# A projection in two halves with a PSUM bank of its own, and unread matrix products at four places, in a network of attention, two Sobel layers and a recurrence

## The chip, the cores and the metric

The kernel runs on one core of one Trainium2 chip. The metric is the device time of one execution in microseconds (us). A core has five engines that run side by side and wait for each other through semaphores: TensorE (PE) multiplies matrices and writes only into PSUM, VectorE (DVE) and ScalarE (ACT) work element by element and can read PSUM, GpSimd (POOL) works element by element but only in SBUF, and SyncE (SP) issues transfers. Each engine takes its instructions in the order in which they stand in the program. TensorE's clock can be granted at full or at half speed.

## The reference, cut to what matters

The input is one image of 256 x 256 pixels with 32 channels. Four layers follow each other; each takes the group norm of the running sum and adds its result to it.

```python
x = x + attention(group_norm(x))     # layer 0
x = x + sobel(group_norm(x))         # layer 1
x = x + sobel(group_norm(x))         # layer 2
x = x + recurrence(group_norm(x))    # layer 3

# layer 0: the axis that is attended over has length 1, so the softmax is 1
mn = layer_norm(m) * ln_gamma + ln_beta       # over the 32 channels
v = mn @ Wv                                   # 32 -> 256
g = sigmoid(mn @ Wg)                          # 32 -> 256
out = (g * v) @ Wo + bo                       # 256 -> 32

# layers 1, 2: 3x3 mean, the two Sobel gradients, root of the sum of squares
out = sqrt(grad_x**2 + grad_y**2 + 1e-6)
```

Layer 3 runs a two-layer gated recurrence of 128 units over 256 columns, for 256 rows at once.

## The kernel before

**Layout.** `xa` and `xb` hold the image in SBUF as 64 blocks of 128 partitions (4 columns of pixels by 32 channels) by 256 rows of pixels. Two neighbouring blocks are a pair of 128 x 512 values, which fills one PSUM bank as fp32; there are 32 pairs (`NST`) and eight banks. An fp32 matrix product appears in the trace as two passes, each with its own weight load.

**Unread products.** At several places the kernel multiplies the identity with a constant tile and never reads the result (`junk`, `px`): `busy` (line 139) in the group norm, line 271 and line 296 in the layer norm, and `busy` (line 921) ahead of the recurrence.

**Layer norm (lines 232 to 298).** First the values are centred and their variances gathered into one bank. Then the reciprocal root `rstd` has to be spread over the channels: for each of the 32 pairs a product `pb` (line 278) takes one of four groups of 32 partitions of `rstd` and fills a bank. `pairs` goes round the four groups, so that neighbouring products lie in different row groups of TensorE. DVE multiplies (line 285), then ACT and POOL in turn apply gamma and beta (lines 287 and 291). The pool `ps_sp` has eight banks; behind the last pair stand four unread products of 256 columns.

**Attention (lines 303 to 366).** The order is written out by hand (`tc.manual_schedule`). For a pair `i` and a half `u % 2` of the 256 hidden channels, each of the four pixel columns `j` needs a value product `pv` and a gate product `pg`. Both take 32 rows of TensorE, those of column `j`. `together` issues two `pv` products and two `pg` products of a later half, then the two sigmoids on ACT (line 328) and the two multiplications `o = pv * sg` on DVE (line 331). It is called twice for each `u`, four times for each pair. The pools are rings: `ps_g` and `ps_v` have four banks each, and a product waits until the bank that it takes over has been read. After the four calls of pair `i`, `project(i - 1)` multiplies the eight `o` tiles of the pair before with `Wo`: for each half four products of 32 columns side by side, added up in one bank, which it takes from the ring of `pg`. ACT adds the bias (line 345), POOL adds the result into `xa` (line 347), and DVE later takes statistics of it (line 350).

**Sobel layers (lines 380 to 538).** Each step of a pair has a due time in a list; the list is sorted and worked off in that order. For a pair `k` the products are `centre` and `edges` (for each of the two gradients `which`), into the tiles `pg0` and `pg1` of the pool `ps_s`, three banks each. Then follow `square`, `total`, `root`, `residual` and `statistics`. Behind each layer stands a `group_norm`: DVE combines the statistics, TensorE makes two small products (`pm`, `pv`) with unread ones around them, and the result is the scale and bias of the next layer.

**Recurrence.** It too is sorted by due times: `project` for step 0 at -1e5, then `busy` with six unread products at -1e4, then step after step with a period of 8.4.

Of the kernel before, what the change touches and what calls it, by code (L numbers as in the profile page):

```python
# [10 lines left out]
F32 = mybir.dt.float32  # L11
# [3 lines left out]
PSUM = bass.MemoryType.PSUM  # L15

S = 256
T = 256
C = 32
J = 4  # L20
NB = T // J
P = 128
# [36 lines left out]
def net_kernel(  # L59
# [20 lines left out]
    nc = tc.nc  # L80
# [13 lines left out]
    ident = cp.tile([P, P], F32, name="ident")  # L94
    make_identity(nc, ident)
    kt = cp.tile([P, NK, P], F32, name="kt")
# [31 lines left out]
    wo = cp.tile([P, D // P, C], F32, name="wo")  # L128
    nc.gpsimd.dma_start(out=wo, in_=w_o.rearrange("(k p) c -> p k c", p=P))

    NST = NB // 2
# [62 lines left out]
    with tc.tile_pool(name="nat", bufs=3) as natp, tc.tile_pool(  # L194
        name="ps_in", bufs=4, space=PSUM
# [31 lines left out]
    pairs = [(g * KS + ks, g, ks) for ks in range(KS) for g in range(4)]  # L227
# [4 lines left out]
    with tc.tile_pool(name="ln", bufs=4) as lnp:  # L232
        rstd = lnp.tile([P, 2 * S], F32, name="rstd", bufs=1)
        with tc.tile_pool(name="ps_ln", bufs=6, space=PSUM) as ps_ln, tc.tile_pool(
            name="ps_var", bufs=1, space=PSUM
        ) as ps_var:
            cen = lnp.tile([P, P], F32, name="cen", bufs=1)
            nc.vector.tensor_scalar(cen, kt[:, K_CEN, :], gn[0], None, ALU.mult)
            pcb = ps_var.tile([P, 1], F32, name="pcb")
            nc.tensor.matmul(pcb, lhsT=kt[:, K_CEN, :], rhs=gn[1], start=True, stop=True)  # L240
            cb = lnp.tile([P, 1], F32, name="cb", bufs=1)
            nc.vector.tensor_copy(cb, pcb)
            pvar = ps_var.tile([P, 2 * S], F32, name="pvar")
            sqs = {}

            def variance(k, g, ks):
                nc.tensor.matmul(
                    pvar[g * C : (g + 1) * C, :],
                    lhsT=avg[:, ks].rearrange("p k j -> p (k j)"),
                    rhs=sqs.pop(k),  # L250
                    start=ks == 0,
                    stop=ks == KS - 1,
                )

            for i, (k, g, ks) in enumerate(pairs):
                pc = ps_ln.tile([P, 2 * S], F32, name="pc")
                nc.tensor.matmul(pc, lhsT=cen, rhs=pair(xa, k), start=True, stop=True)
                sqs[k] = lnp.tile([P, 2 * S], F32, name="sq", bufs=10)
                nc.scalar.activation(sqs[k], pc, AF.Square, bias=cb)
                nc.vector.tensor_scalar(pair(xb, k), pc, cb, None, ALU.add)  # L260
                if g == 3 and ks:
                    for q in pairs[i - 7 : i - 3]:
                        variance(*q)
            for q in pairs[-4:]:
                variance(*q)
            std = lnp.tile([P, 2 * S], F32, name="std", bufs=1)
            nc.scalar.activation(std, pvar, AF.Sqrt, bias=ln_eps)
            table(AF.Sigmoid, std[:, 0:1])
            nc.vector.reciprocal(rstd, std)
            for _ in range(9):  # L270
                nc.tensor.matmul(
                    pvar[:, 0:S], lhsT=ident, rhs=kt[:, 0:2, :], start=True, stop=True
                )
        with tc.tile_pool(name="ps_sp", bufs=8, space=PSUM) as ps_sp:
            for i, (k, g, ks) in enumerate(pairs):
                rows = slice(g * C, (g + 1) * C)
                pb = ps_sp.tile([P, 2 * S], F32, name="pb")
                nc.tensor.matmul(
                    pb,
                    lhsT=spread[rows, ks * J : (ks + 1) * J, :].rearrange("p j c -> p (j c)"),  # L280
                    rhs=rstd[rows, :],
                    start=True,
                    stop=True,
                )
                nc.vector.tensor_mul(pair(xb, k), pair(xb, k), pb)
                if i % 2:
                    nc.scalar.activation(
                        pair(xb, k), pair(xb, k), AF.Identity, scale=gamma4, bias=beta4
                    )
                else:  # L290
                    nc.gpsimd.tensor_scalar(
                        pair(xb, k), pair(xb, k), gamma4, beta4, ALU.mult, ALU.add
                    )
            junk = ps_sp.tile([P, 2 * S], F32, name="pb")
            for _ in range(4):
                nc.tensor.matmul(
                    junk[:, 0:S], lhsT=ident, rhs=kt[:, 0:2, :], start=True, stop=True
                )

    stats = new_stats()
    with tc.tile_pool(name="at", bufs=3) as atp, tc.tile_pool(
        name="ps_g", bufs=4, space=PSUM
    ) as ps_g, tc.tile_pool(name="ps_v", bufs=4, space=PSUM) as ps_v:
        gates, gated = {}, {}

        def inner(w, u, j, ps):
            i, half = divmod(u, 2)
            k = pairs[i][0]  # L310
            rows = slice(j * C, (j + 1) * C)
            mn = xb[rows, 2 * k : 2 * k + 2, :].rearrange("p b s -> p (b s)")
            nc.tensor.matmul(  # L313
                ps, lhsT=w[rows, half * P : (half + 1) * P], rhs=mn, start=True, stop=True
            )
            return ps

        def together(values, gates_of):

            pvs = {k: inner(wv4, *k, ps_v.tile([P, 2 * S], F32, name="pv")) for k in values}  # L320
            pgs = {
                k: inner(wg4, *k, ps_g.tile([P, 2 * S], F32, name="pg"))
                for k in gates_of
                if k[0] < 2 * NST
            }
            for k, pg in pgs.items():
                gates[k] = sg = atp.tile([P, 2 * S], F32, name="sg", bufs=8)
                nc.scalar.activation(sg, pg, AF.Sigmoid)  # L328
            for k, pv in pvs.items():
                gated[k] = o = atp.tile([P, 2 * S], F32, name="o", bufs=17)  # L330
                nc.vector.tensor_mul(o, pv, gates.pop(k))  # L331

        def project(i):
            po = ps_g.tile([P, 2 * S], F32, name="pg")
            for half in range(2):
                for j in range(J):
                    nc.tensor.matmul(
                        po[j * C : (j + 1) * C, :],
                        lhsT=wo[:, half, :],
                        rhs=gated.pop((2 * i + half, j)),  # L340
                        start=half == 0,
                        stop=half == 1,
                    )
            r = atp.tile([P, 2 * S], F32, name="r", bufs=2)
            nc.scalar.activation(r, po, AF.Identity, bias=bo4)
            dst = pair(xa, pairs[i][0])
            nc.gpsimd.tensor_add(dst, dst, r)

        def statistics(i):
            nc.vector.bn_stats(stats[:, i, :], pair(xa, pairs[i][0]))  # L350

        with tc.manual_schedule():
            together((), [(0, j) for j in range(J)])
            together((), [(1, j) for j in range(2)])
            for i in range(NST):
                for u in (2 * i, 2 * i + 1):
                    if i >= 3 and u % 2:
                        statistics(i - 3)
                    together([(u, 0), (u, 1)], [(u + 1, 2), (u + 1, 3)])
                    together([(u, 2), (u, 3)], [(u + 2, 0), (u + 2, 1)])  # L360
                if i >= 1:
                    project(i - 1)
            table(AF.Sqrt, one)
            for i in range(NST - 1, NST):
                project(i)
            for i in range(NST - 3, NST):
                statistics(i)
    lw = ctx.enter_context(tc.tile_pool(name="lw", bufs=1))
# [11 lines left out]
    def sobel_layer(src, dst, scale, bias, between):  # L380
# [152 lines left out]
        with tc.manual_schedule():  # L533
            for _, k, part, args in todo:
                part(k, *args)
                if part is statistics and between:
                    between.pop(0)(lambda: flat(ps_s.tile([P, 2, S], F32, name="pg1")))
        stack.close()
# [239 lines left out]
def recurrence(tc, out, ident, weights, inputs, general):  # L778
# [39 lines left out]
    def at(when, what, *args):  # L818
        todo.append((when, len(todo), what, args))

    def project(l, h, t):

        if t >= T:
            return
        zz = v["zz", l, h] = ps_zz.tile([P, 4 * H], F32, name=f"zz{l}{h}")
        rows = slice(l * X1, l * X1 + KX)
        x = inputs.of(t, rows, slice(h * P, (h + 1) * P))
        nc.tensor.matmul(zz, lhsT=x, rhs=fx[rows, l, :], start=True, stop=l == 0 and t == 0)  # L828
# [125 lines left out]
        at(((k - inputs.NX + 1) * inputs.XT * J + 2.0) * PERIOD, inputs.load, k)  # L954
    for h in range(2):
        at(-1e5, project, 0, h, 0)
    at(-1e4, busy, 6)
    at(PLAN[1, 1]["x"] - PERIOD, project, 0, 0, 1)
    at(PLAN[1, 1]["x"] - PERIOD, busy, 2)
    for t in range(T):  # L960
# [52 lines left out]
```

## Time and profile before

| What | us |
| --- | --- |
| Median of three runs (2828.97 to 2829.38) | 2829.04 |
| The profiled execution | 2832.39 |
| its span, first to last instruction | 2830.50 |
| load and transposition, first group norm (0 to 38) | 38.0 |
| layer norm up to the spreading (38 to 82) | 44.0 |
| layer norm, spreading (82 to 103.5) | 21.5 |
| attention, up to the next group norm (103.5 to 323.9) | 220.4 |
| group norm and first Sobel layer (323.9 to 473) | 149.1 |
| group norm and second Sobel layer (473 to 619.9) | 146.9 |
| group norm and weights of the recurrence (619.9 to 629.6) | 9.7 |
| recurrence (629.6 to 2830.5) | 2200.9 |

The profile is that of one execution, so its own time is shown beside its span; the difference is what lies before the first and behind the last instruction. An engine is busy while one of its instructions runs. Overlapping instructions of one engine count once, and TensorE's passes overlap, so that a PE that is busy all the time need not work at its peak. The granted clock is a share of full speed. In a timeline each line gives the start, the time that the group of equal instructions covers, engine, line, operation, the tiles written and read, the number, and in brackets the idle time of the engine before it with what ended it.

### The profile page before, as it was taken

What the parts mean: (1) busy time and instruction counts of PE and PEld (TensorE: products, weight loads), DVE (VectorE), ACT (ScalarE), POOL (GpSimd) and SP (SyncE); (2) the same over time, 40 slices, a digit from 0 to 9 for tenths busy, and PEclk for the clock granted to TensorE, in tenths of its full rate; (3) what the DMA queues carried; (4) which work ended last, traced back from release to release, by engine and by line L of the source; (5) the groups of instructions that cost most, each with busy time, mean ns of one, the idle gap of its engine ahead of it and who ended that gap; (6) DMA issues with size and microseconds to landing.
All of it is one profiled execution on the core that took longest, in us unless ns stands there. A gap on an engine that the chain in (4) does not pass through costs nothing.

```text
span 2830.5 us, 38940 instructions
## 1 busy us (share of the span) xinstructions
PE 2785.1 (98%) x9709; PEld 1051.1 (37%) x9709; DVE 2494.4 (88%) x7272; ACT 2379.3 (84%) x6980; POOL 1299.9 (46%) x1295
## 2 busy tenths in 40 slices
PE   7999999999999999999999999999999999999998
PEld 4433434343333333333333333333333333333332
DVE  6788798978999999999999999999999999999997
ACT  5677676768988888888888888888888888888887
POOL 2211375654444444444444444444444444444443
PEclk9899999999999999999999999999999999999999
DMA  3000000010000000000000000000000000000000
GB/s 136 1 1 1 16 1 1 1 23 6 16 12 12 12 12 12 12 12 12 12 14 12 12 12 12 12 12 12 12 12 12 12 12 14 16 15 12 5 5 8
DMA packets 94337, 38.41 MB, mean 14 GB/s; under 512 B 74852, under 2 KB 91269, under 8 KB 94104
## 3 DMA queue, kind: packets, MB, share of 16 engines
q1 hardware_dynamic: 92612, 34.61, 5.3%
q8 instruction: 82, 1.34, 0.2%
q14 instruction: 151, 1.24, 0.1%
q10 hardware_dynamic: 692, 0.93, 0.1%
q0 software_dynamic: 800, 0.30, 0.0%
HBM read 10.63 MB, written 8.39 MB: 7 GB/s over the span
## 4 chain that ended last, share of the span: by engine, by line
PE 76%; DVE 1%; ACT 0%; issue 0%; POOL 0%; DVEq 0%; POOLq 0%; ACTq 0%
PE zz L853 34%; PE zz L828 19%; PE zz L848 15%; PE pt L910 5%; PE px L933 1%; PE px L930 1%; DVE ve L866 0%; PE px L924 0%; POOL rs L869 0%; ACT sq L861 0%; ACT ga L842 0%; DVE c L890 0%; DVE h L905 0%; DVE fc L894 0%; DVE c L898 0%
## 5 line engine op out<-in xcount | busy, mean ns | idle before, releaser
L869 POOL TENSOR_TENSOR rs<-ve,mhalf 128x4 f32<-128x4 f32 x1024 | 1037.5, 1013 | 1153.5 <-DVE ve L866 1153.5
L853 PE MATMUL zz<-wc,hT 128*128 128x512 f32 x2040 | 1100.3, 621 | 0.5 <-DVE hT L914 0.5
L842 ACT ACTIVATE ga<-zz,rs 128x128 f32<-128x128 f32 x3072 | 927.1, 366 | 32.0 <-POOL rs L869 13.1
L866 DVE TENSOR_REDUCE ve<-sq 128x4 f32<-128x516 f32 x1024 | 707.2, 691 | 123.8 <-ACT sq L861 61.1
L861 ACT ACTIVATE sq<-zz 128x512 f32<-128x512 f32 x1024 | 609.4, 595 | 126.4 <-PE zz L853 116.1
L828 PE MATMUL zz<-fx,xt 33*128 33x512 f32 x2048 | 583.1, 642 | 0.5 <-DVE e L710 0.5
L853 PEld LDWEIGHTS zz<-wc,hT 128*128 128x128 f32 x2040 | 324.0, 188 | 554.3 <-DVE c L898 288.1
L848 PE MATMUL zz<-wc,hT 128*128 128x512 f32 x1024 | 525.0, 594 | 0.0
L902 ACT ACTIVATE th<-c 128x128 f32<-128x128 f32 x1024 | 318.1, 311 | 89.9 <-DVE c L898 80.8
L842 ACT ACTIVATE go<-zz,rs 128x128 f32<-128x128 f32 x1024 | 390.4, 381 | 0.0
L890 DVE TENSOR_TENSOR c<-ga 128x128 f32<-128x128 f32 x1024 | 295.8, 289 | 39.2 <-ACT ga L842 25.2
L910 PEld LDWEIGHTS pt<-ident,h 128*128 128x128 f32 x1024 | 142.8, 139 | 502.1 <-DVE h L905 501.5
L914 DVE COPY hT<-pt 128x128 f32<-128x128 f32 x1024 | 292.6, 286 | 26.0 <-PE pt L910 4.0
L910 PE MATMUL pt<-ident,h 128*128 128x128 f32 x1024 | 299.5, 292 | 8.1 <-DVE h L905 8.1
L905 DVE TENSOR_TENSOR h<-go,th 128x128 f32<-128x128 f32 x1024 | 291.9, 285 | 11.8 <-ACT th L902 1.5
L894 DVE TENSOR_TENSOR fc<-ga,c 128x128 f32<-128x128 f32 x1020 | 297.5, 292 | 0.6 <-ACT ga L842 0.6
L898 DVE TENSOR_TENSOR c<-c,fc 128x128 f32<-128x128 f32 x1020 | 288.1, 282 | 6.8
L828 PEld LDWEIGHTS zz<-fx,xt 33*128 33x128 f32 x2048 | 156.3, 185 | 258.9 <-ACT go L842 193.7
L331 DVE TENSOR_TENSOR o<-pv,sg 128x512 f32<-128x512 f32 x256 | 158.1, 681 | 43.6 <-PE pg L313 37.7
L848 PEld LDWEIGHTS zz<-wc,hT 128*128 128x128 f32 x1024 | 162.3, 198 | 70.8 <-issue 40.8
L328 ACT ACTIVATE sg<-pg 128x512 f32<-128x512 f32 x256 | 138.6, 599 | 31.4 <-PE pg L313 26.7
L313 PE MATMUL pv<-xb,wv 32*128 32x512 f32 x512 | 156.5, 620 | 0.0
(154 smaller groups left out, 2174.5 us busy)
## 6 DMA issues: line engine op xcount, KB each, us to landing
xt<-xa SPq DMA_DIRECT2D x256, 64.0 KB, 2.0
nat<-in_x_dram SPq DMA_DIRECT2D x16, 512.0 KB, 7.9
out_dram<-st SPq DMA_DIRECT2D x254, 32.0 KB, 1.6
wc<-in_L_conv_W_cell_dram SPq DMA_DIRECT2D x2, 512.0 KB, 4.4
kt<-in_consts_dram ACTq DMA_DIRECT2D x1, 832.0 KB, 5.8
wv<-in_L_conv_Wv_dram POOLq DMA_DIRECT2D x4, 32.0 KB, 5.1
wg<-in_L_conv_Wg_dram POOLq DMA_DIRECT2D x4, 32.0 KB, 6.7
gamma<-in_L_conv_ln_gamma_dram POOLq DMA_DIRECT2D x4, 0.1 KB, 5.9
```

Source lines behind the costliest of these rows:

```text
L828: nc.tensor.matmul(zz, lhsT=x, rhs=fx[rows, l, :], start=True, stop=l == 0 and t == 0)
L842: nc.scalar.activation(dst, gates(x, g), func, scale=scale)
L848: nc.tensor.matmul(get("zz"), lhsT=v["hT", 0, t][:, seqs], rhs=wc[:, l, 0, :], start=False, stop=t == 0)
L853: nc.tensor.matmul(get("zz"), lhsT=v["hT", l, t - 1][:, seqs], rhs=wc[:, l, 1, :], start=False, stop=True,)
L861: nc.scalar.activation(sqs[l, h][:, :, 0:H], four(get("zz")), AF.Square, scale=float(H**-0.5))
L866: nc.vector.tensor_reduce(ve, sqs[l, h], AX.X, ALU.add)
L869: nc.gpsimd.tensor_tensor(rs, get("ve"), inputs.mhalf, ALU.pow)
L890: nc.vector.tensor_mul(c, gates(get("ga"), 0), gates(get("ga"), 3))
L894: nc.vector.tensor_mul(fc, gates(get("ga"), 1), get("c"))
L902: nc.scalar.activation(th, get("c"), AF.Tanh)
L910: nc.tensor.transpose(pt[:, 0:P], get("h"), ident)
L914: nc.vector.tensor_copy(v["hT", l, t][:, seqs], get("pt")[:, 0:P])
```

## The change

It does four things.

1. In the layer norm's spreading, the pool `ps_sp` has seven banks, and one bank `junk` stands beside it. Behind each of the last ten `pb` products one unread product of 128 columns is issued. The four unread products of 256 columns behind the last pair are gone.
2. In attention, `project` handles one half per call. The first half takes a tile `po` from a pool of its own with one bank (`ps_o`), the second half adds to it, and then the bias, the addition and the rest follow as before. The calls stand behind the second and the fourth call of `together` of a pair, instead of both halves behind the fourth. `ps_v` has three banks instead of four; `ps_g` keeps four and holds only gate products.
3. In both Sobel layers nine unread products of 256 columns are issued behind the last `edges` of the last pair, in a tile of the ring of `pg1`.
4. Ahead of the recurrence `busy` issues eight unread products instead of six.

```diff
-        with tc.tile_pool(name="ps_sp", bufs=8, space=PSUM) as ps_sp:
+        with tc.tile_pool(name="ps_sp", bufs=7, space=PSUM) as ps_sp:
+            junk = ps_sp.tile([P, 2 * S], F32, name="junk", bufs=1)
...
-            junk = ps_sp.tile([P, 2 * S], F32, name="pb")
-            for _ in range(4):
-                nc.tensor.matmul(
-                    junk[:, 0:S], lhsT=ident, rhs=kt[:, 0:2, :], start=True, stop=True
-                )
+                if i >= len(pairs) - 10:
+                    nc.tensor.matmul(
+                        junk[:, 0:P], lhsT=ident, rhs=kt[:, 0, :], start=True, stop=True
+                    )
...
-    ) as ps_g, tc.tile_pool(name="ps_v", bufs=4, space=PSUM) as ps_v:
+    ) as ps_g, tc.tile_pool(name="ps_v", bufs=3, space=PSUM) as ps_v, tc.tile_pool(
+        name="ps_o", bufs=1, space=PSUM
+    ) as ps_o:
...
-        def project(i):
-            po = ps_g.tile([P, 2 * S], F32, name="pg")
-            for half in range(2):
-                for j in range(J):
-                    nc.tensor.matmul(
-                        po[j * C : (j + 1) * C, :],
-                        lhsT=wo[:, half, :],
-                        rhs=gated.pop((2 * i + half, j)),
-                        start=half == 0,
-                        stop=half == 1,
-                    )
+        def project(i, half):
+
+            if half == 0:
+                gated["po"] = ps_o.tile([P, 2 * S], F32, name="po")
+            po = gated["po"]
+            for j in range(J):
+                nc.tensor.matmul(
+                    po[j * C : (j + 1) * C, :],
+                    lhsT=wo[:, half, :],
+                    rhs=gated.pop((2 * i + half, j)),
+                    start=half == 0,
+                    stop=half == 1,
+                )
+            if half == 0:
+                return
...
                     together([(u, 0), (u, 1)], [(u + 1, 2), (u + 1, 3)])
                     together([(u, 2), (u, 3)], [(u + 2, 0), (u + 2, 1)])
-                if i >= 1:
-                    project(i - 1)
+                    if i >= 1:
+                        project(i - 1, u % 2)
             table(AF.Sqrt, one)
-            for i in range(NST - 1, NST):
-                project(i)
+            for half in range(2):
+                project(NST - 1, half)
...
                 part(k, *args)
+                if part is edges and args == (0,) and k == NST - 1:
+                    junk = flat(ps_s.tile([P, 2, S], F32, name="pg1"))
+                    for _ in range(9):
+                        nc.tensor.matmul(
+                            junk[:, 0:S], lhsT=ident, rhs=kt[:, 0:2, :], start=True, stop=True
+                        )
...
-    at(-1e4, busy, 6)
+    at(-1e4, busy, 8)
```

## The prediction

> **What bounds the kernel now.** I read the page first (part 2), then the table of stretches for each stage the change touches, then the timeline of one attention period, because a mean over the span says nothing of stages with different limits. The recurrence takes 2200.9 of 2830.5 us and the change touches only its first few us, so what can move lies before 630 us. In part 2, and in a table of stretches that I cut where the granted clock changes:
>
> ```profile
> PE   7999999999999999999999999999999999999998
> PEclk9899999999999999999999999999999999999999
> 84.79:88.20 3.41, 3.41 (x14) 1.58 (x12) 3.41 (x7) 2.26 (x4) 2.23 (x4) 1.00 0.01 2
> 88.20:105.27 17.07, 16.96 (x51) 11.29 (x50) 14.17 (x24) 10.43 (x13) 9.37 (x13) 0.50 0.00 1
> 190.22:196.90 6.68, 6.68 (x51) 2.50 (x48) 5.46 (x11) 5.03 (x10) 1.27 (x1) 1.00 0.01 2
> 196.90:203.59 6.69, 6.69 (x51) 2.50 (x49) 5.47 (x11) 5.04 (x10) 1.27 (x1) 1.00 0.00 0
> 473.91:477.32 3.41, 3.41 (x12) 2.62 (x10) 1.25 (x4) 0.00 (x0) 0.00 (x0) 0.50 0.00 0
> 630.92:637.75 6.83, 6.83 (x16) 4.23 (x15) 1.94 (x5) 2.68 (x9) 2.06 (x2) 0.50 0.19 44
> ```
>
> Columns: stretch, its length, busy time of PE, weight loads, DVE, ACT, POOL, then the granted clock. PE shows as busy nearly everywhere, and still has half its clock in the layer norm's spreading stage (88.2 to 105.3), after the first Sobel layer (473.9) and at the start of the recurrence (630.9). In attention the clock is full; a period (one pair of blocks) is 6.68 us, DVE busy 5.46 of it, ACT 5.03. So neither of those bounds it, and a "busy" PE proves nothing. The timeline of a period:
>
> ```profile
> 192.08 0.70 PE L313 MATMUL pv<-xb,wv 32*128 32x512 f32 x2
> 193.30 2.48 DVE L331 TENSOR_TENSOR o<-pv,sg 128x512 f32<-128x512 f32 x4 [1.22 <-PE pg L313]
> 194.05 0.29 PEld L313 LDWEIGHTS pv<-xb,wv 32*128 32x128 f32 x2 [0.74 <-DVE o L331]
> 194.65 0.18 PEld L313 LDWEIGHTS pv<-xb,wv 32*128 32x128 f32 x1 [0.30 <-DVE o L331]
> ...
> 196.91 1.92 PE L337 MATMUL pg<-o,wo 128*32 128x512 f32 x16
> 198.76 0.70 PE L313 MATMUL pv<-xb,wv 32*128 32x512 f32 x2
> ...
> 199.99 2.48 DVE L331 TENSOR_TENSOR o<-pv,sg 128x512 f32<-128x512 f32 x4 [1.22 <-PE pg L313]
> ```
>
> I call one call of `together` a round: two pv and two pg products. It is read as a chain. Round 1's products start at 192.08, its first multiply at 193.30 (**1.23** from product to multiply). Round 3's first product waits for that multiply's bank and starts at 194.05 (**0.745** from multiply to freed bank), its second at 194.65, one multiply later (0.598). Round 4 ends the loop, the projection starts at 196.91 and round 1 again at 198.76. DVE then idles 1.22. So the loop is: ring of four pv banks, two rounds deep, then the projection in one piece.
>
> **What the skill says.** "PSUM — Partial Sum Buffer", section Specifications (TRN2): eight banks of 512 fp32. So 4+4 can only become 4+3+1, and the projection's own bank is taken from pv. The DVE waits above show what a missing bank costs. "TensorE: Matmul & The Clock Gate", Part 2: only weight loads are pulled ahead, "The MATMULs themselves stay in program order"; so one waiting product stops all behind it. The trace agrees: in the instruction list round 3's pg products start 7 ns after its late second pv (194.654 after 194.647). The same page, Part 3: products in different row groups run side by side. Agrees: round 1's four products start within 20 ns. Part 1 there: the clock follows how busy the array was in windows of 3.4 us. Partly: half clock begins and ends in steps of 3.41, but the spreading stage lost it while PE shows 3.41 of 3.41 busy; its products fill 32 rows of 128. What counts seems to be the filled part of the array.
>
> **Part by part.**
>
> *Attention.* The built order of the changed kernel shows what each product waits for: with three banks, the second pv of every round waits for the first multiply of the round just before it; now it waits for one two rounds back. That adds a wait to every round 2 and 4, and behind it in PE's order stand the round's two pg products, then the projection's half, then the next round. Half a period now runs: round 1 to its first multiply 1.23, to the freed bank 0.745, that late product and the two pg behind it until the projection can start 1.06 (195.842 to 196.904 in the list), one half of the projection until round 3 starts 1.00 (0.88 from the first to the third group of passes, plus 0.11 for the change of weights before round 1). Sum 4.03; the period 8.07 against 6.68: +1.38. The projection's starts stand at 116.69 and 317.51 with 30 periods between: +41.5. The first pair, without projection, +1.2 (two halves of 1.23 + 0.745 + 0.97 = 2.95, against the 4.67 from its first pv at 107.19 to 4.83 before the first projection). At the end one half of pair 30's projection has moved into the loop: -1. DVE needs about 8 x 0.598 + 0.61 = 5.4 per period, so what the halves spare it is idle time anyway; the evacuation by ACT and the addition on POOL stay as many.
>
> *Layer norm.* Ten unread 128-column products go between the last ten spreading products (pb), four of 256 columns behind them go. Until now DVE sets the pace there: nine multiplies in 5.46 us, 0.598 each, the last at 101.69; pb hides because four row groups run side by side. A full-array product between them ends that. At half clock a 256-column pass takes 0.427 (L296), so pb costs 2 x 0.854 = 1.71 and the unread one 0.43: at least 2.14 per pair if no switch costs anything, at most 2.72 with 0.29 for each of two switches (0.13 gap and 0.16 longer first pass, seen from the last pb to L296). I take 2.43. The cover DVE gave is gone: 2.43 against 0.598. With seven banks product 22 waits for multiply 15 and can start at 92.87 (92.12 + 0.745). The last multiply starts at 92.87 + 9 x 2.43 + 2.17 (from a pb to its multiply at half clock) = 116.9, and attention, which waits for it, at 117.65 instead of 103.53: +14.1 (bounds +11.5 and +16.7). The clock should not come back there: serial, the ten fill (1.71/4 + 0.43)/2.43 = 35% of the array. Windows with four row groups side by side at 71% did not bring it back. Attention's first rounds then start at half clock for longer than the 1.7 us of now: +2 (0 to +6).
>
> *Sobel.* Nine unread products fill PE from the last edges (about 470 and 617 us) for 9 x 0.43 = 3.9 us, beside ACT's and DVE's last root, residual and statistics. The clock should stay full. Now the norm's second small product starts 1.07 us after its input is ready (q ends 475.91, pv 476.98), behind two unread products at half clock. New: they end near 473.9, three more run 1.3, the first small product starts 0.3 to 0.4 later than now, the second about at once. Net -0.65 per layer, -1.3.
>
> *Recurrence.* Two more unread products before step 0: at half clock +1.7 on the path (the first transpose at 637.23 waits for them, its input ended 636.43), at full clock -0.8. Which, depends on where the windows fall: +0.5.
>
> Sum: 14.1 + 2 + 41.5 + 1.2 - 1 - 1.3 + 0.5 = +57.0. The profiled execution took 2832.39 us with a span of 2830.50; on it that gives 2889.4. The runs' median is 2829.04, 3.35 less, so the time is **2886**.
>
> **Rivals.**
> 1. *The clock comes back among the layer norm's products.* For it: 2.14 of every 2.43 us PE streams something. Against: the 71% above. At full clock a pair costs 1.27: attention starts at 92.87 + 9 x 1.27 + 1.15 + 0.75 = 106.2, +2.7, and gains 1 at its start: in all 57 - 14.1 - 2 + 2.7 - 1 = +42.6, 2872.
> 2. *The third bank is enough* (not slower). The place is the second pv of rounds 2 and 4. If its bank is free when PE arrives, half a period is two rounds and one half: 0.96 + 1.06 + 1.00 = 3.02, a period 6.04, -0.64 x 31 = -19.8 in place of +41.7: -4.5, **2824.5**. It decides from a period of 6.2 on, where the other terms are paid. For it: it needs only the pace of DVE (5.4). Against: 1.23 + 0.745 between a product and its freed bank are both in the timeline above, and DVE would have to be 1 us sooner.
> 3. *Attention loses the clock.* Its filled share falls from 77% (5.16 of 6.68: four rounds of 0.86 and 1.72 for the projection) to 64%. Against: the Sobel layers keep the clock with about 59% (per pair four full passes and ten of a quarter array, 0.43 each, in 149.1/32 = 4.66 us). At half clock half a period is 2.1 + 0.745 + 1.95 + 1.9 = 6.7; for 8 of 31 pairs that is +43: 2929.
>
> **How the numbers follow.** Forecast 66% (its own range 2877 to 2897: layer norm 2.5 either way, 0.1 us per period, the start), rival 1 14%, rival 2 11%, rival 3 6%, and 3% for what I don't see. The range 2868 to 2900 takes in the forecast and rival 1. 0.2% is 5.7 us, about what can be told from no change here. Rival 2 lies at that edge: faster 8%, same 3%, slower 89%.
>
> **What would show it.** Right: a period of 8.0 to 8.1 in attention with one DVE wait of pv in each of rounds 2 and 4, DVE idle about 2.6 per period; ten pb and unread products in turn at half clock, attention's first product near 117; full clock behind both Sobel layers. Wrong: a period at or under 6.7, or pb still paced by DVE at 0.6 to the end.

## The result, and the profile after

| | before | after |
| --- | --- | --- |
| Median of four runs each, us | 2829.21 (2828.97 to 2831.77) | 2897.72 (2896.00 to 2899.70) |
| The profiled execution | 2832.39 | 2896.00 |
| its span | 2830.50 | 2894.20 |
| spreading, first `pb` to attention's first product | 21.5 | 38.5 |
| attention, first product to the projection's last pass | 219.0 | 267.4 |
| a period of attention | 6.68 | 8.12 |
| half clock around the spreading | 88.20 to 105.27 | 85.95 to 130.32 |

The changed kernel takes 1.024 times as long (95% interval 1.0223 to 1.0258). The page of the changed kernel, parts 2 and 5 (part 5: busy time and mean ns of one, then the idle time ahead of the group and what ended it), and behind it the same two groups in the kernel before:

```profile
PE   8999999999999999999999999999999999999998
PEclk9699999999999999999999999999999999999999
...
L333 DVE TENSOR_TENSOR o<-pv,sg 128x512 f32<-128x512 f32 x256 | 165.0, 686 | 82.1 <-PE pg L315 67.8
L330 ACT ACTIVATE sg<-pg 128x512 f32<-128x512 f32 x256 | 138.8, 595 | 99.7 <-PE pg L315 97.7
```

```profile
L331 DVE TENSOR_TENSOR o<-pv,sg 128x512 f32<-128x512 f32 x256 | 158.1, 681 | 43.6 <-PE pg L313 37.7
L328 ACT ACTIVATE sg<-pg 128x512 f32<-128x512 f32 x256 | 138.6, 599 | 31.4 <-PE pg L313 26.7
```

PE still looks busy everywhere, but the second slice (about 72 to 145 us) shows a clock of 0.6 where it was 0.8. DVE and ACT stand idle 82 and 100 us ahead of attention's multiplications and sigmoids, where it was 44 and 31, and nearly all of it is spent waiting for products. The table of stretches says where (length, then busy time of PE, weight loads, DVE, ACT, POOL, and the granted clock):

```profile
85.95:130.32 44.37, 43.42 (x96) 19.49 (x94) 18.39 (x30) 16.56 (x25) 9.46 (x13) 0.50 0.00 0
130.32:385.70 255.38, 254.54 (x1504) 73.88 (x1503) 180.41 (x282) 154.71 (x278) 39.38 (x31) 1.00 0.00 1
690.11:700.35 10.24, 9.79 (x19) 5.12 (x18) 2.70 (x7) 2.97 (x8) 1.64 (x2) 0.50 0.23 52
```

The clock is halved through the end of the spreading and the first 12 us of attention, and full for the rest of attention. So the long periods are not throttling. The timeline of one half of a period, in the changed kernel:

```profile
231.74 1.06 PE L341 MATMUL po<-o,wo 128*32 128x512 f32 x8
232.73 0.70 PE L315 MATMUL pv<-xb,wv 32*128 32x512 f32 x2
...
233.96 2.67 DVE L333 TENSOR_TENSOR o<-pv,sg 128x512 f32<-128x512 f32 x4 [0.86 <-PE pg L315]
...
234.70 0.18 PEld L315 LDWEIGHTS pv<-xb,wv 32*128 32x128 f32 x1 [0.81 <-DVE o L333]
234.71 0.70 PE L315 MATMUL pg<-xb,wg 32*128 32x512 f32 x2
...
235.77 1.06 PE L341 MATMUL po<-o,wo 128*32 128x512 f32 x8
...
236.77 0.70 PE L315 MATMUL pv<-xb,wv 32*128 32x512 f32 x2
```

Round 1 starts at 232.73, its first multiplication 1.23 later at 233.96; the second `pv` of round 2 starts at 234.70, 0.74 later, because it takes the bank that this multiplication has just given back. The gate products follow it at 234.71, the next half of the projection at 235.77, the next round 1.00 later. The wait that stood at one place in the period now stands in each half of it: 4.03 us from half to half. In the trace every fourth half comes after 4.13, which makes the mean period 8.12.

The spreading, from where the alternation has not begun to its end, in the same timeline:

```profile
89.37 5.46 DVE L286 TENSOR_TENSOR xb<-xb,pb 128x512 f32<-128x512 f32 x9
...
112.51 2.07 PE L279 MATMUL pb<-rstd,spread 32*128 32x512 f32 x2
...
114.52 0.80 PE L296 MATMUL junk<-kt,ident 128*128 128x128 f32 x2
114.62 0.69 DVE L286 TENSOR_TENSOR xb<-xb,pb 128x512 f32<-128x512 f32 x1 [2.04 <-PE pb L279]
115.24 2.07 PE L279 MATMUL pb<-rstd,spread 32*128 32x512 f32 x2
117.24 0.80 PE L296 MATMUL junk<-kt,ident 128*128 128x128 f32 x2
117.35 0.69 DVE L286 TENSOR_TENSOR xb<-xb,pb 128x512 f32<-128x512 f32 x1 [2.04 <-PE pb L279]
118.29 2.09 PE L315 MATMUL pg<-xb,wg 32*128 32x512 f32 x8 [0.26 <-PE junk L296]
```

One small product and one unread one alternate, 2.73 us per pair (112.51 to 115.24), and DVE waits 2.04 us for each product. Up to 94.8 it multiplied without a break (nine in 5.46 us from 89.37).

### The profile page after: what moved, and what is told of

It is laid out like the page before. It is cut to its first block, busy times and chain, and to the rows that moved or that the text cites. A ratio compares the mean times of both kernels' runs of the same rounds, so it can differ in the third digit from the quotient of the medians.

```text
span 2894.2 us, 39046 instructions
## 1 busy us (share of the span) xinstructions
PE 2855.8 (99%) x9761; PEld 1055.6 (36%) x9761; DVE 2506.0 (87%) x7272; ACT 2378.5 (82%) x6980; POOL 1300.1 (45%) x1295
## 4 chain that ended last, share of the span: by engine, by line
PE 75%; DVE 0%; ACT 0%; POOL 0%; issue 0%; DVEq 0%; POOLq 0%; ACTq 0%
PE zz L865 34%; PE zz L840 19%; PE zz L860 15%; PE pt L922 5%; PE px L945 1%; PE px L942 1%; PE px L936 0%; POOL rs L881 0%; DVE ve L878 0%; ACT ga L854 0%; ACT sq L873 0%; DVE h L917 0%; DVE c L902 0%; DVE fc L906 0%; DVE c L910 0%
## 5 line engine op out<-in xcount | busy, mean ns | idle before, releaser
L333 DVE TENSOR_TENSOR o<-pv,sg 128x512 f32<-128x512 f32 x256 | 165.0, 686 | 82.1 <-PE pg L315 67.8
L315 PE MATMUL pv<-xb,wv 32*128 32x512 f32 x512 | 199.3, 638 | 0.8 <-DVE o L333 0.8
```

## The experiments

The theory: three `pv` banks cost about 46 us in attention, the alternation in the spreading about 19 with the attention's slow start, the Sobel layers and the recurrence's lead-in nothing that can be measured. Rivals: that attention is long because of the clock it inherits, that the halving is the cost, that the layer norm's loss is hidden later. A ratio is to the kernel before, run on the same chip, with its 95% interval; stages are read from the profiled execution of each.

| Kernel | us | ratio (interval) | spreading | period |
| --- | --- | --- | --- | --- |
| e1 after, attention as before | 2848.8 | 1.0070 (1.0053 to 1.0087) | 38.5 | 6.68 |
| e2 after, spreading as before | 2875.3 | 1.0163 (1.0147 to 1.0180) | 21.1 | 8.12 |
| e3 before, halves, 4 `pv` 3 `pg` 1 `po` | 2865.4 | 1.0128 (1.0111 to 1.0144) | 21.1 | 7.88 |
| e4 before, halves adjacent, 4 `pv` 4 `pg` | 2827.2 | 0.9996 (0.9987 to 1.0004) | 21.4 | 6.70 |
| e5 before, whole, 3 `pv` 4 `pg` 1 `po` | 2872.8 | 1.0147 (1.0132 to 1.0163) | 21.5 | 8.06 |
| e6 before, unread products of 32 rows | 2831.2 | 1.0005 (0.9997 to 1.0014) | 21.2 | 6.69 |
| e7 before, unread products behind | 2831.1 | 1.0002 (0.9994 to 1.0011) | 23.0 | 6.69 |
| e8 before, Sobel and lead-in alone | 2830.0 | 0.9999 (0.9990 to 1.0007) | 21.4 | 6.69 |
| e9 before, seven behind Sobel | 2824.6 | 0.9982 (0.9976 to 0.9989) | 21.5 | 6.68 |
| e10 e4 and e9 together | 2824.4 | 0.9981 (0.9975 to 0.9988) | 21.5 | 6.70 |
| e11 before, halves apart, 4 `pv` 4 `pg` | 2836.0 (one run) | | 21.5 | 6.92 |

### Taking the change apart: e1 and e2

e1 is the changed kernel with the attention's pools and `project` of the kernel before:

```diff
-        name="ps_g", bufs=4, space=PSUM
-    ) as ps_g, tc.tile_pool(name="ps_v", bufs=3, space=PSUM) as ps_v, tc.tile_pool(
-        name="ps_o", bufs=1, space=PSUM
-    ) as ps_o:
+        name="ps_g", bufs=4, space=PSUM
+    ) as ps_g, tc.tile_pool(name="ps_v", bufs=4, space=PSUM) as ps_v:
...
-                    if i >= 1:
-                        project(i - 1, u % 2)
+                if i >= 1:
+                    project(i - 1)
```

> The changed kernel with only the attention as it was (4 gate banks that the projection shares, 4 value banks, both halves of the projection in one go). Theory: the missing value bank is worth 1.4 us per pair, so the attention's period goes back to 6.68 us and the time to the kernel before plus the layer norm's loss (16.9 by the two traces) plus 1 to 6 for an attention that starts at half clock: 2847 to 2853. Rival, that the attention is long because it starts behind a throttled layer norm and not because of its banks: the period stays near 8 and the time near 2895.

2848.8, with a period of 6.68 behind a spreading of 38.5 us. The attention recovers fully although it starts at half clock, so its length is its own.

e2 is the changed kernel with the spreading of the kernel before:

```diff
-        with tc.tile_pool(name="ps_sp", bufs=7, space=PSUM) as ps_sp:
-            junk = ps_sp.tile([P, 2 * S], F32, name="junk", bufs=1)
+        with tc.tile_pool(name="ps_sp", bufs=8, space=PSUM) as ps_sp:
...
-                if i >= len(pairs) - 10:
-                    nc.tensor.matmul(
-                        junk[:, 0:P], lhsT=ident, rhs=kt[:, 0, :], start=True, stop=True
-                    )
+            junk = ps_sp.tile([P, 2 * S], F32, name="pb")
+            for _ in range(4):
+                nc.tensor.matmul(
+                    junk[:, 0:S], lhsT=ident, rhs=kt[:, 0:2, :], start=True, stop=True
+                )
```

> The changed kernel with only the layer norm's spreading as it was (8 banks, four trailing unread products). Theory: spreading takes 21.5 us again instead of 38.5, the attention starts at full clock within 2 us of its start, and the period stays at 8.1: 2897.7 - 16.9 - about 3 = 2878, between 2874 and 2882. Rival, that what the layer norm loses is hidden by the attention (POOL and ACT catch up later): about 2895.

2875.3. The half clock ends at 101.85, 0.7 us ahead of the attention's first product (102.56). From that product to the first half of the projection it takes 11.50 us; in the changed kernel, with the same loop, 16.05. So the slow start costs 4.55 us. The period is 8.12 although attention starts at full clock: the clock that it inherits doesn't make it long. The two losses over the kernel before, 19.0 (e1) and 45.5 (e2), add up to 64.5 of the 68.5. A slow start costs more with three banks than with four: with four the whole attention takes 219.5 us in e1 and 216.5 in e8, where it runs at full clock throughout, so 3.0 against 4.55. That is 1.5 of the missing 4.0; the other 2.5 lie within the two intervals (each about 5 us either way).

### Which part of the attention's edit: e3, e4, e5, e11

e3 takes the projection's bank from the gates and not from the values. The diff is against the changed kernel's attention; all else is the kernel before:

```diff
-        name="ps_g", bufs=4, space=PSUM
-    ) as ps_g, tc.tile_pool(name="ps_v", bufs=3, space=PSUM) as ps_v, tc.tile_pool(
+        name="ps_g", bufs=3, space=PSUM
+    ) as ps_g, tc.tile_pool(name="ps_v", bufs=4, space=PSUM) as ps_v, tc.tile_pool(
```

> The kernel before with the projection in halves and its own bank, but the bank is taken from the gates (3) and not from the values (4). Theory: either ring of three makes the fourth product wait for a read out of the first, since gates and values alternate two by two; period about 8.0 us, time 2829 + 30 x 1.35 = 2870, between 2862 and 2876. Rival, that it is the value's ring alone, because VectorE's multiplication is later than ScalarE's sigmoid: period 6.7 to 7.1, time 2829 to 2842.

2865.4 and a period of 7.88, two halves of 3.94. Either ring of three costs nearly the same, so the rival that only the values' ring matters falls.

e4 halves the projection without a bank of its own: the halves stand behind the third and the fourth round, and `po` is a tile of the gates' ring.

```diff
-                if i >= 1:
-                    project(i - 1)
+                    if i >= 1 and u % 2:
+                        project(i - 1, 0)
                     together([(u, 2), (u, 3)], [(u + 2, 0), (u + 2, 1)])
+                    if i >= 1 and u % 2:
+                        project(i - 1, 1)
```

> The kernel before with the projection in halves (behind the third and the fourth round of a pair), no bank of its own: it stays in the gates' ring of 4, and the values keep 4. Theory, that the banks and not the halving cost the time: a second change from small products to the pass of the projection per pair costs about 0.2 us, 30 x 0.2 = 6, time 2835, between 2829 and 2842. Rival, that a pass in halves is itself the cost (the row groups stop and start twice, the multiplications are waited for twice): period near 8, time near 2870.

2827.2. Two first halves of the projection, a period apart:

```profile
199.43 1.06 PE L339 MATMUL pg<-o,wo 128*32 128x512 f32 x8
...
206.13 1.07 PE L339 MATMUL pg<-o,wo 128*32 128x512 f32 x8
```

The period is 6.70, against 6.68 before (6.696 and 6.685 as means over 25 periods). So the halving is all but free where the halves stand close together; the 6 us that I had put for a second change to the projection's pass did not come. The time's interval takes in no change, so it isn't called a gain.

e5 is the other corner: the projection whole, but in its own bank.

```diff
-    ) as ps_g, tc.tile_pool(name="ps_v", bufs=4, space=PSUM) as ps_v:
+    ) as ps_g, tc.tile_pool(name="ps_v", bufs=3, space=PSUM) as ps_v, tc.tile_pool(
+        name="ps_o", bufs=1, space=PSUM
+    ) as ps_o:
...
-            po = ps_g.tile([P, 2 * S], F32, name="pg")
+            po = ps_o.tile([P, 2 * S], F32, name="po")
```

> The kernel before with the projection whole as it was, but in a bank of its own taken from the values (3 value banks, 4 gate banks, 1 for the projection). Theory: the bank is the cost, whole or in halves; period near 8.0 to 8.3, time 2829 + 30 x 1.4 = 2871, between 2865 and 2880. Rival, that it takes both, the halves and the smaller ring, since a half stands between every four products: period under 7.3, time under 2848.

2872.8, period 8.06. The bank alone costs what the changed kernel's attention costs; halves neither cause it nor cure it.

e11 puts the halves where the changed kernel has them, with `po` out of the gates' ring of four (the diff is that of `project` in the change, with `ps_g.tile(..., name="pg")` for `ps_o.tile(..., name="po")` and both pools at 4).

> The kernel before with the projection in halves behind the second and the fourth round as in the changed kernel, but without a bank of its own: it takes one of the gates' four when its first half is issued and gives it back after the second is read, some two rounds of the four later. Theory, that it is the banks left to the rounds which set the period: the rounds between the halves run with three gate banks, 3.9 us, and the others with four, about 3.3; period 7.2 to 7.7, time 2829 + 30 x 0.75 = 2851, between 2843 and 2860. Rival, that only a bank that is set apart costs: period 6.6 to 6.8, time 2826 to 2833.

2836.0 and a period of 6.92, between the two expectations, and its timeline shows why:

```profile
200.85 1.07 PE L339 MATMUL pg<-o,wo 128*32 128x512 f32 x8
...
202.04 0.69 ACT L349 ACTIVATE r<-pg,bo 128x512 f32<-128x512 f32 x1 [0.49 <-PE pg L339]
...
203.83 1.07 PE L339 MATMUL pg<-o,wo 128*32 128x512 f32 x8
...
207.77 1.07 PE L339 MATMUL pg<-o,wo 128*32 128x512 f32 x8
```

The pass at 200.85 is a second half: ACT reads the result at 202.04, and from 202.73 the bank is back in the ring. From that pass to the next first half (203.83) it is 2.98 us. From the first half to the second (207.77) the projection holds the bank: 3.94. I had expected 3.3 and 3.9. So the ring one bank short costs 0.96 us in the half of a period in which it is short; where the bank comes back in time a half runs in 2.98.

### The spreading: e6 and e7

e6 leaves the ten unread products among the last `pb` ones, and their bank, but each takes 32 rows. This diff and the next are against the changed kernel's spreading; all else is the kernel before:

```diff
-                        junk[:, 0:P], lhsT=ident, rhs=kt[:, 0, :], start=True, stop=True
+                        junk[:, 0:P], lhsT=ident[0:C, :], rhs=kt[0:C, 0, :], start=True, stop=True
```

> The kernel before with the layer norm's ten unread products and their bank, but each product takes 32 rows (the first row group) and not 128, so that it is of the same kind as the small products around it. Theory, that it is the switch to a product over all rows that takes the small products one by one: spreading near 22 us, between 21 and 24, time 2829 to 2832. Rival, that ten more products and a ring of seven banks cost what they cost whatever their shape: spreading over 30 us, time near 2848.

2831.2, spreading 21.2. Lines of its timeline:

```profile
94.05 0.42 PE L296 MATMUL junk<-kt,ident 32*128 32x128 f32 x1
94.05 1.22 PE L279 MATMUL pb<-rstd,spread 32*128 32x512 f32 x1
94.26 0.63 PE L296 MATMUL junk<-kt,ident 32*128 32x128 f32 x2
...
94.48 1.22 PE L279 MATMUL pb<-rstd,spread 32*128 32x512 f32 x1
```

An unread and a small product start together at 94.05, and DVE multiplies without a break (11 in 6.67 us from 89.48). Same number of products, same bank, same place: what costs 17 us is that the unread ones took all rows. But these do not bring the clock back: it stays at half until 108.98, against 105.27 in the kernel before.

e7 keeps the products over all rows and their bank and puts all ten behind the last `pb`:

```diff
-                if i >= len(pairs) - 10:
-                    nc.tensor.matmul(
-                        junk[:, 0:P], lhsT=ident, rhs=kt[:, 0, :], start=True, stop=True
-                    )
+            for _ in range(10):
+                nc.tensor.matmul(
+                    junk[:, 0:P], lhsT=ident, rhs=kt[:, 0, :], start=True, stop=True
+                )
```

> The kernel before with the ten unread products over all 128 rows and their bank, but all ten behind the last small product and none among them. Theory, that the alternation is the cost: spreading 21 to 23 us, the clock comes back near where it does in the kernel before, time 2828 to 2833. Rival, that the ring of seven banks makes the small products wait: spreading 26 or more, time over 2834.

2831.1, spreading 23.0. The unread products in the kernel before, then in e7 with attention's first product:

```profile
99.64 3.78 PE L296 MATMUL pb<-kt,ident 128*128 128x256 f32 x8
```

```profile
98.00 4.63 PE L296 MATMUL junk<-kt,ident 128*128 128x128 f32 x20
102.74 1.66 PE L313 MATMUL pg<-xb,wg 32*128 32x512 f32 x8
```

Of the 1.5 us, 0.85 are the ten products, which take 4.63 where the four took 3.78. The other 0.6 are the ring of seven: the unread products begin 18.25 us behind the first `pb` where it was 17.64, one multiplication later. The ratio can't tell either kernel from the one before.

The two also show what ended the half clock. In e7 it ends 1.1 us behind attention's first product, and in the nine kernels here that keep the four unread products behind the last pair it ends between 0.7 ahead of that product and 2.1 behind it. In the three that have no such run of products over all rows it lasts 7.9 us (e6), 8.5 (e1) and 12.0 (the changed kernel) into attention. So by these kernels the slow start comes from taking the four products away: neither the ten in turn with `pb` nor the ten of 32 rows stand in for them.

### The small parts: e8, e9, e10

e8 is the kernel before with only the nine products behind each Sobel layer and the eight ahead of the recurrence, as in the change's last two parts.

> The kernel before with only the nine unread products behind each Sobel layer and eight instead of six ahead of the recurrence. Theory by the two traces: full clock behind both layers gives the last product 1.1 us and the waiting statistics' product loses as much, so nothing that can be measured: 2827 to 2831. Rival by the recorded working, 0.65 gained per layer: 2827.7, which this run can't tell from nothing by its time, so the layers' stretches are read from the trace. Rival that the drop of the clock moves into the recurrence: up to 2834.

2830.0, no change that can be measured. Inside the layers there is one. In the timelines of the two kernels, first the one before, then the changed one, behind the first Sobel layer:

```profile
473.60 1.02 DVE L153 BATCH_NORM_AGGREGATE mv<-stats 128x2 f32<-128x192 f32 x1
474.79 0.48 PE L156 MATMUL pm<-mv,kt 128*128 128x1 f32 x2
475.69 0.22 DVE L163 SCALAR_TENSOR_TENSOR q<-d,mv 128x1 f32<-128x1 f32 x1
476.98 0.42 PE L165 MATMUL pv<-q,kt 128*128 128x1 f32 x2
477.73 0.16 DVE L170 RECIPROCAL scale<-std 128x1 f32<-128x1 f32 x1 [1.82 <-ACT std L168]
```

```profile
536.39 1.02 DVE L153 BATCH_NORM_AGGREGATE mv<-stats 128x2 f32<-128x192 f32 x1
536.89 1.56 PE L143 MATMUL junk<-kt,ident 128*128 128x256 f32 x6
538.29 0.28 PE L156 MATMUL pm<-mv,kt 128*128 128x1 f32 x2
538.99 0.22 DVE L163 SCALAR_TENSOR_TENSOR q<-d,mv 128x1 f32<-128x1 f32 x1
539.48 0.28 PE L165 MATMUL pv<-q,kt 128*128 128x1 f32 x2
540.09 0.16 DVE L170 RECIPROCAL scale<-std 128x1 f32<-128x1 f32 x1 [0.88 <-ACT std L168]
```

The mean and variance `mv` are there at 474.62 and at 537.41, the scale starts at 477.73 and at 540.09: 3.11 and 2.68. The second small product `pv` no longer waits (0.27 behind `q` instead of 1.07), but the first, `pm`, now waits 0.88 behind three more unread products that can only start when the nine are done. In all four profiles with nine products it is 2.68 in both layers, without them between 2.9 and 3.95. The 0.43 of the second layer does not reach the recurrence: from that layer's `mv` to the recurrence's first product it takes 8.10 in e1 and 8.07 in e2, and 8.10 in the kernel before. Why is not settled. The 0.43 of the first layer is too little to be seen in the runs' times.

So two products fewer should let `pm` go at once. e9 is the kernel before with seven behind each layer and the lead-in left alone:

```diff
+                if part is edges and args == (0,) and k == NST - 1:
+                    junk = flat(ps_s.tile([P, 2, S], F32, name="pg1"))
+                    for _ in range(7):
+                        nc.tensor.matmul(
+                            junk[:, 0:S], lhsT=ident, rhs=kt[:, 0:2, :], start=True, stop=True
+                        )
```

> The kernel before with unread products behind each Sobel layer, seven and not nine (the recurrence's lead-in keeps its six). With nine, the time from a layer's mean and variance to its scale was 2.68 us in every profile, of which 0.88 was the statistics' first product waiting for the last of the unread ones; without them it was 3.0 to 3.9. Theory: two fewer end 0.86 earlier, so the product goes at once and the clock stays full: 1.8 to 1.9 us per layer, 1.2 to 1.3 less than before in each, time 2827 (2825 to 2830). Rival, that seven are too few to hold the clock: the drop is back, 3.1 us per layer, time 2830.

2824.6, just under the range, and the only single edit here that is faster, by 0.2 per cent: 0.9982 (0.9976 to 0.9989). Its timeline:

```profile
471.55 1.56 PE L143 MATMUL junk<-kt,ident 128*128 128x256 f32 x6
471.91 1.02 DVE L153 BATCH_NORM_AGGREGATE mv<-stats 128x2 f32<-128x192 f32 x1
472.99 0.38 PE L156 MATMUL pm<-mv,kt 128*128 128x1 f32 x2
473.80 0.22 DVE L163 SCALAR_TENSOR_TENSOR q<-d,mv 128x1 f32<-128x1 f32 x1
474.18 0.28 PE L165 MATMUL pv<-q,kt 128*128 128x1 f32 x2
474.79 0.16 DVE L170 RECIPROCAL scale<-std 128x1 f32<-128x1 f32 x1 [0.77 <-ACT std L168]
```

The last three unread products start at 471.55, `mv` is ready at 472.93 and `pm` goes at 472.99; the scale comes 1.86 us behind `mv` and the clock is full. That is 1.25 per layer. The rest of the 5.2 is not settled: 0.6 of it is the stretch between the second layer's scale and the recurrence's first product in this one profile.

e10 is e4 and e9 in one kernel.

> Both that may gain: the projection in halves behind the third and fourth round within the gates' four banks (2.2 us less attention in its profile) and seven unread products behind each Sobel layer (1.2 per layer). Theory: the gains add, 2829.8 - 2.2 - 2.5 = 2825, between 2822 and 2828. Rival, that the drops of the clock which are kept out of the Sobel layers come in the recurrence's lead-in and take the gain back: 2828 to 2831.

2824.4, the same as e9, so the gains don't add. In its profile attention is 1.2 us shorter than in e9, with 2.1 us at half clock instead of 5.2, and the recurrence 1.3 longer. The 2.2 us that e4's profile seemed to gain were of the same kind: its attention (216.8) ran at full clock throughout, as that of e8 did with the projection whole (216.5). By these runs the halving is worth nothing, and e9 is the version that beats both kernels.

## Why the prediction was right, and where its sizes were off

Direction and causes held, and the stated range held the time. The forecast was 11.7 us low; its own range, 2877 to 2897, missed by 0.7. On the profiled execution the sum was +57.0; the stages of the two traces give:

| Step | forecast | measured | where it is read |
| --- | --- | --- | --- |
| layer norm | +14.1 | +16.9 | 38.46 against 21.53 |
| attention's start at half clock | +2 | +4.5 | 16.05 against e2's 11.50 to the first half |
| 30 periods | +41.5 | +43.0 | 30 x (8.119 - 6.685) |
| first pair, end of the loop | +0.2 | +1.0 | the rest of attention's +48.5 |
| Sobel layers | -1.3 | +0.1 | end of attention to the recurrence's first product |
| recurrence and its end | +0.5 | +0.4 | first product to the last write of `st` -0.2, behind it +0.6 |
| sum | +57.0 | +65.9 | |

Before the spreading the changed kernel's profile is 2.15 us ahead; that stretch starts between 79.8 and 82.0 in the profiles here with no edit ahead of it, and is not the change. 65.9 - 2.15 leaves the 63.6 between the two profiled executions. The other 4.9 to the medians' 68.5 is that one profiled execution lies 3.2 above its median and the other 1.7 below.

**Attention** was the main step and stands as put: one wait of a `pv` product per half, all four terms of the half within 0.01 us, clock full, DVE idle in every half. e5 shows that the missing bank does it alone, e4 that the halves need cost nothing. The 4.13 of every fourth half was not foreseen; its cause isn't settled. The small row "first pair, end of the loop" hides two slips of the sum and a third thing that nearly cancels them. The sum left out the rounds of the second pair, which stand ahead of the 30 periods and run with three banks too: from attention's first product to the second pair's projection (its second half in e2) it takes 15.5 us in e2 and 12.3 in e8, both at full clock, so +3.2 and not +1.2; and the -1 at the end came as +0.3. Against these +3.5 stand 2.5 us that the profiled attention of the kernel before lost to 5.1 us at half clock (219.0 against e8's 216.5). That +1.0 is near +0.2 is luck.

**Layer norm.** The step was right, with the wrong value taken between its own bounds. The term is the price of a switch between a small product and one over all rows: I took half of 0.29 each, and the full 0.29 is paid both times (2 x 0.854 + 0.43 + 2 x 0.29 = 2.72; measured 2.73: 2.00 from `pb` to the unread product and 0.73 back). Nine steps at 0.30 more are 2.7 of the 2.8. The page "TensorEngine Tiling (Array Packing)" of the Trainium skill, section Tiling Modes, speaks for a full price at each switch, though it gives no figure: a change of the tiling mode, not just of the tile, drains the engine. e6 agrees as far as it goes: the same ten products in the same mode leave the spreading at 21.2 us, in the other they make it 38.5. It doesn't show that the 0.29 is the drain. In the changed kernel the weights of the unread product also begin to load only with its first pass (both at 92.70), and no run separates the two.

**The start.** The half clock lasted 12.0 us into attention, where I allowed for little more than now. The cost was inside the bounds (0 to +6), but the reason was missed: the working counted the four unread products behind the last pair only as time saved, and they were what ended the half clock near attention's start (e7 and the nine kernels that keep them).

**Sobel.** The mechanism held (full clock behind both layers) and its size nearly, -0.43 instead of -0.65 per layer, as `pm` waits 0.7 longer (0.88 against 0.17) and not the 0.3 to 0.4 that I put. It doesn't show in the total. The second layer's share did not reach the recurrence (e1, e2), and in the changed kernel's profile a drop of the clock at 690.11 also falls ahead of the recurrence: 9.06 us from the second layer's `mv` to the first product of the recurrence, against 8.10 before.

**Recurrence.** That +0.4 is near +0.5 is luck as well. The drop fell where the two products added stand: the first transpose comes 9.1 us behind the recurrence's first product where it was 7.7, and the recurrence behind it was 1.6 shorter.

**The rivals.** The clock did not come back in the spreading (half through to 130.32), and attention did not lose it. "The third bank is enough" gave a half period of 3.02: e11 shows it, 2.98, in the half in which the bank comes back in time. The arithmetic was right and its condition not met, as three banks aren't enough for the 1.23 + 0.745 from a product to its free bank.

## What to carry to other kernels

A pool of banks has a length in time: the time from a product to its freed bank, against the time until the ring comes round. Work that out before a bank is taken away for something else, and count a bank as gone only while it is held. An unread product over all rows should stand where no small products run side by side, since it ends their overlap. Making it small is no way out: those of 32 rows did not lengthen the spreading here, but did nothing for the clock either (e6), while a run over all rows behind the last `pb` ended the half clock (e7). And it must end before the next product that matters is ready, or it gives back what the clock gained.

## What the runs showed of the hardware that was not expected

- A change from 32-row products to one over all 128 rows and back costs 0.29 us each way at half clock, beside the passes themselves (2.73 per pair). At full clock two more changes per pair of blocks cost 0.01 us (e4: 6.696 against 6.685).
- Products of 32 rows, up to four side by side and with ten more of them added, did not restore the clock: half until 108.98 in e6 while PE was busy 22.04 of those 23.89 us. "TensorE: Matmul & The Clock Gate" of the skill, Part 1, ties the clock to how busy the engine has been; with busy as the profile counts it, that does not fit here. The prediction's guess, the filled share of the array, isn't settled either: by its own estimates 71% in the spreading did not bring the clock back, while the Sobel layers keep it with 59%.
- Stretches of the same code differ by some us between profiles as drops of the clock fall: in six profiles with an unchanged loop and the same period attention took 216.5 us (e8), 217.0 (e7), 219.0 (before, e9), 219.5 (e1) and 221.0 (e6), with 0, 1.1, 5.1 and 5.2, 8.5 and 11.3 us of it at half clock. Edits of a microsecond must be read inside their stage.
